# A four-stage transformer stack on one core: stages without barriers, ordered by one list scheduler, with query and key stacks made by products

## The chip, the cores and the metric

The kernel runs on one core of one Trainium2 chip. The metric is the device time of one execution in microseconds (us). A core has a matrix engine (TensorE; PE in the profile, PEld for its weight loads), VectorE (DVE), ScalarE (ACT), GpSimd (POOL) and SyncE (SP, which here only issues DMAs). Each engine works through its own instructions in the order in which the build put them, and waits where one of them waits.

## The reference

Input x is (4, 512, 128) in fp32. Four residual layers follow each other; each batch of 512 tokens (a "block") is independent of the others but for the experts' capacity, which counts tokens over all blocks.

```
x = x + attention(layernorm(x)) @ WO        # 16 heads of 8, causal softmax
x = x + moe(layernorm(x))                   # 8 experts, 2 of them per token, 128 -> 512 -> 128, gelu, capacity
y = layernorm(x) with gain and shift        # recurrence, of layernorm(x) again
state = sigmoid(decay) * state + k * v      #   1024 channels, along the 512 tokens
x2 = xn + (sigmoid(g) * q * state / 8) @ Wo + bo
x = x + x2 + gelu(layernorm(x2) @ W1 + b1) @ W2 + b2
out = x + ternary(layernorm(x))             # silu(w1 y) * (w2 y), two gelu layers of 512x512, w3
```

(xn is layernorm(x); the last layer's weights are −1, 0 or 1 and have a scale for each output.)

## The kernel before, in words

The work of a block is cut into stages, each a Python generator that issues a piece of work at every step and yields an estimate of its cost in us. They are, for a block b:

- `project(b)`: layernorm, four transposes, then the query and key products (`pqk`, one of [128 x 512] each). For the scores the values are wanted as a high and a low part (`hl`, L197 and L198), and stacked by groups of four heads at 32 rows each. The stacking is done by DMA: four DMAs write the parts to DRAM (`rows_q`, `rows_k`, L201) and eight read them back as `qs` and `ks` (L207, L208).
- `maxima(g)`, for each of four head groups: scores on TensorE, the causal mask added by a product with an identity, maxima on VectorE (`mx`, L244), split into two parts (`mh`, L251 and L252) and transposed (`pm`, `mT`).
- `Weights.group(g)`: the scores again with the maxima subtracted by a product with `spread`, exp on ScalarE (`ex`, L283), the diagonal tiles masked on GpSimd (L288), and the products with the values (`po`). `finish` copies `po` (`oT`, L306), transposes it and divides.
- `output(b)`: the product with WO, added to `xs`. `route(b)`: layernorm, router product, the two best experts, each token's row in a buffer of 8 x 192 seats (`rt_at`, L430), and eight indirect DMAs on GpSimd that scatter the tokens to `xgd` in DRAM (L434).
- `experts(b)`: loads `xgd` (`xg`, L472), 12 transposes, then 8 experts of two layers (`ph`, `hT`, `py`, `xoT`), weights loaded through three buffers (`ew`); the results go to DRAM (`ygd`, L500); after a yield of 4.0 eight indirect gathers fetch them (`got`, L536), and after a yield of 6.0 eight VectorE instructions add them to `xs` (L544).
- `recurrence(b)`: two layernorms, then eight channel chunks of four products (`pp`), a scan along the tokens (L605) and an output product (`por`). Its five matrices stay in SBUF (`lk`, `lv`, `lg`, `lq`, `lo`, 512 KB each).
- `feed(b)` and `ternary(b)`: the two feed-forward layers. `ternary` splits its inputs into a high and a low part (`hh`, `hl`, L683 and L684). `round_weights` converts the ternary weights once and looks for values that are not exact (L752 to L760).

The order of instructions comes from `weave`, which takes the next step of whichever of two or three generators has the least estimated time behind it. Stages are woven within two kinds of phase. The experts phase of block b holds experts(b), feed and ternary of block b−1 (for b = 0 `round_weights`) and the maxima of block b+1. The weights phase holds recurrence(b) beside weights, output and route of block b+1 and project(b+2). Each phase opens a tile pool of its own (`phase()`), whose buffers reuse the space of the phase before: a first user of such a buffer waits for the last user of that space. DMAs are issued on SP in program order; scatters and gathers on GpSimd.

TensorE's products and transposes are issued by two helpers, so their lines in the profile are L64 and L67 throughout. The word "(3 forms)" in a group's row means that the shapes differ within it.

Of the kernel before, what the change touches and what calls it, by code (L numbers as in the profile page):

```python
# [20 lines left out]
P = 128  # L21
# [22 lines left out]
def block_kernel(ctx: ExitStack, tc: tile.TileContext, i: dict, out: bass.AP):  # L44
    nc = tc.nc

    const = ctx.enter_context(tc.tile_pool(name="const", bufs=1))
    state = ctx.enter_context(tc.tile_pool(name="state", bufs=1))
    wpool = ctx.enter_context(tc.tile_pool(name="wpool", bufs=1))
    small = ctx.enter_context(tc.tile_pool(name="small", bufs=4))  # L50
    work = ctx.enter_context(ExitStack())
    ypool = work.enter_context(tc.tile_pool(name="ypool", bufs=2))
    att = work.enter_context(tc.tile_pool(name="att", bufs=2))
    stk = work.enter_context(tc.tile_pool(name="stk", bufs=1))
    ew = work.enter_context(tc.tile_pool(name="ew", bufs=3))
    rt = work.enter_context(tc.tile_pool(name="rt", bufs=1))
    scr = work.enter_context(tc.tile_pool(name="scr", bufs=NB, space=DRAM))
    ps_s = work.enter_context(tc.tile_pool(name="ps_s", bufs=2, space=PSUM))
    ps_o = work.enter_context(tc.tile_pool(name="ps_o", bufs=1, space=PSUM))
    ps_d = work.enter_context(tc.tile_pool(name="ps_d", bufs=2, space=PSUM))  # L60
# [8 lines left out]
    class At:  # L69
        pass  # L70

    At.ypool, At.ps_d, At.ew, At.scr = ypool, ps_d, ew, scr

    def bank(name, tag="pt", shape=(P, S)):

        return At.ps_d.tile(list(shape), F32, tag=tag, name=name, bufs=2 if tag == "pt" else 1)
# [18 lines left out]
    mhalf = const.tile([P, TB], F32, name="mhalf")  # L95
# [4 lines left out]
    make_identity(nc, identb)  # L100

# [8 lines left out]
    def layernorm(src, dst):  # L110

        st = small.tile([P, TB, 6], F32, tag="ln_st", name="ln_st")
        mv = small.tile([P, TB, 2], F32, tag="ln_mv", name="ln_mv")
        ve = small.tile([P, TB], F32, tag="ln_ve", name="ln_ve")
        rs = small.tile([P, TB], F32, tag="ln_rs", name="ln_rs")
        for t in range(TB):
            nc.vector.bn_stats(st[:, t, :], src[:, t, :])
        for t in range(TB):
            nc.vector.bn_aggr(mv[:, t, :], st[:, t, :])
        nc.vector.tensor_scalar(ve, mv[:, :, 1], EPS, None, ALU.add)  # L120
        nc.gpsimd.tensor_tensor(rs, ve, mhalf, ALU.pow)  # L121
        for t in range(TB):
            nc.vector.tensor_scalar(
                dst[:, t, :], src[:, t, :], mv[:, t, 0:1], rs[:, t : t + 1],
                ALU.subtract, ALU.mult,
            )

# [10 lines left out]
    def normed(src):  # L138
        y = At.ypool.tile([P, TB, D], F32, tag="y", name="y")
        layernorm(src, y)  # L140
        return y

    def turned(y, gain=None, shift=None):

        yT = At.ypool.tile([P, S], F32, tag="yT", name="yT", bufs=3)
# [6 lines left out]

    def run(stage):
        for _ in stage:
            pass

    def weave(*streams):

        live = [[0.0, n, stage, stretch] for n, (stage, stretch) in enumerate(streams)]
        while live:  # L160
            first = min(live, key=lambda x: x[:2])
            took = next(first[2], None)
            if took is None:
                live.remove(first)
            else:
                first[0] += took * first[3]
# [8 lines left out]
    qs = [stk.tile([P, S], F32R, name=f"qs{g}") for g in range(NG)]  # L175
    ks = [stk.tile([P, S], F32R, name=f"ks{g}") for g in range(NG)]

    mhs = [stk.tile([P, TB, NG, HP], F32R, name=f"mh{x}") for x in range(2)]

    spread = stk.tile([P, P], F32R, name="spread")  # L180

    vs = stk.tile([P, TB, H0, HP], F32, name="vs")

    def project(b, big):

        y = normed(blk(xs, b))
        yield 5.0
        yT = turned(y)
        yield 1.5
        pqk = ps_s.tile([P, 2, S], F32, tag="s", name="pqk")  # L190
        mm(pqk[:, 0, :], lhsT=wq, rhs=yT, start=True, stop=True)
        yield 0.9
        mm(pqk[:, 1, :], lhsT=wk, rhs=yT, start=True, stop=True)
        hl = big.tile([P, 2, 2, S], F32R, tag="hl", name="hl", bufs=1)
        rows = []
        for x, n in enumerate("qk"):
            nc.scalar.copy(hl[:, x, 0, :], pqk[:, x, :])  # L197
            nc.vector.tensor_tensor(hl[:, x, 1, :], pqk[:, x, :], hl[:, x, 0, :], ALU.subtract)  # L198
            d = scr.tile([P, 2, 2, S], F32, tag=f"rows_{n}", name=f"rows_{n}")
            for half in range(2):  # L200
                nc.sync.dma_start(  # L201
                    d[:, half] if n == "q" else d[:, :, half],
                    hl[:, x, half].bitcast(F32).unsqueeze(1).to_broadcast([P, 2, S]),
                )
            rows.append(d.rearrange("(g h) a b s -> g (h a b) s", g=NG))
        for g in range(NG):
            nc.sync.dma_start(qs[g].bitcast(F32), rows[0][g])  # L207
            nc.sync.dma_start(ks[g].bitcast(F32), rows[1][g])  # L208
        yield 0.9
# [4 lines left out]
        yield 1.0  # L214
# [11 lines left out]
    def maxima(g):  # L226

        mx = att.tile([P, TB, NG], F32, tag="mx", name="mx")
        for part in ((3,), (2,), (1, 0)):
            pq = quad()  # L230
            at = 0
            for t in part:
                product(pq, qs[g][:, ts(t, P)], ks[g], 0, (t + 1) * P, at, start=(at == 0))
                at += (t + 1) * P
            at = 0
            for t in part:
                for h in range(NG):
                    mm(pq[h // 2][:, h % 2, at + t * P : at + (t + 1) * P], lhsT=identb, rhs=mask_q,
                       start=False, stop=True, skip_group_check=True)
                at += (t + 1) * P  # L240
            at = 0
            for t in part:
                for pr in range(2):
                    nc.vector.tensor_reduce(  # L244
                        mx[:, t, ts(pr, 2)], pq[pr][:, :, at : at + (t + 1) * P], AX.X, ALU.max,
                        negate=True,
                    )
                at += (t + 1) * P
            yield 1.6
        mh = mhs[g % 2]  # L250
        nc.vector.tensor_copy(mh[..., 0], mx)  # L251
        nc.vector.tensor_tensor(mh[..., 1], mx, mh[..., 0], ALU.subtract)  # L252
        yield 1.0
        pm = bank("pm", shape=(P, TB, P))
        for t in range(TB):
            transpose(pm[:, t, :], mh[:, t].rearrange("p h r -> p (h r)").bitcast(F32))
        mT = mTs[g] = att.tile([P, S], F32R, tag="mT", name="mT", bufs=NG)
        nc.scalar.copy(mT, flat(pm))
        yield 0.5

    mTs = {}

    class Weights:


        def __init__(self, big):
            self.big, self.late = big, None
            self.o = att.tile([P, TB, D], F32, tag="o", name="o", bufs=1)

        def group(self, g):  # L270
            po = ps_o.tile([P, S], F32, tag="po", name="po")
            exs = {}

            def unit(part):
                pq = quad()
                at = 0
                for t in part:
                    product(pq, ks[g][:, ts(t, P)], qs[g], t * P, S, at, start=(at == 0))
                    product(pq, spread, mTs[g], t * P, S, at)
                    at += S - t * P  # L280
                for pr in range(2):
                    ex = self.big.tile([P, 2, S], F32, tag="ex", name="ex", bufs=4)
                    nc.scalar.activation(ex[:, :, :at], pq[pr][:, :, :at], AF.Exp, scale=scale0)  # L283

                    step = S - part[0] * P
                    e = ex.rearrange("p j (i n) -> p j i n", n=step if len(part) > 1 else S)
                    e = e[:, :, : len(part), 0:P]
                    nc.gpsimd.affine_select(  # L288
                        out=e, in_=e, compare_op=ALU.is_ge, fill=0.0, base=0,
                        pattern=[[0, 2], [0, len(part)], [1, P]], channel_multiplier=-1,  # L290
                    )
                    at = 0
                    for t in part:
                        exs[t, pr] = ex[:, :, at : at + S - t * P]
                        at += S - t * P

            def values(t):
                for h in range(NG):
                    mm(po[ts(h, HP), t * P :], lhsT=vs[:, t, NG * g + h, :],
                       rhs=exs[t, h // 2][:, h % 2, :], start=(t == 0), stop=(t == TB - 1))  # L300

            def finish():
                values(2)
                values(3)
                oT = att.tile([P, S], F32, tag="oT", name="oT", bufs=1)
                nc.scalar.copy(oT, po)  # L306
                yield 2.0
                pt = flip(tiles(oT)).rearrange("p t (h r) -> p t h r", r=HP)
# [664 lines left out]
```

## Time and profile before

| | |
|---|---|
| time, median of 4 runs | 899.92 us (895.85 to 900.70) |
| the profiled execution: its own time | 907.21 us |
| its span, from the first to the last instruction | 905.1 us |
| mean granted TensorE clock | 0.824 |
| TensorE busy | 645.9 us (71%) |
| TensorE weight loads | 367.2 us (41%) |
| VectorE busy | 424.7 us (47%) |
| ScalarE busy | 276.7 us (31%) |
| GpSimd busy | 170.0 us (19%) |
| moved by DMA | 56.85 MB, 63 GB/s over the span |

The busy time of an engine counts its arithmetic only. The chain is the sequence of work that ended last, followed back from the last instruction; its shares add up to the span. A line such as "L244 DVE ... mx<-s" names the kernel's line, the engine, and which buffer was made from which. A wait is written as who waited, for whom, the total in us, how often, and the longest.

### The profile page before, as it was taken

Reading aid. Unit: us, or ns where it says so; the run is one execution under the profiler, and the core shown is the slowest. Engines: PE = TensorE matmul, PEld = TensorE weight load, DVE = VectorE, ACT = ScalarE, POOL = GpSimd, SP = SyncE. Lnnn points to the kernel's source line nnn. Section 1 sums busy time; section 2 is a strip of 40 time slices with the busy share of each in tenths; the row PEclk is TensorE's granted clock in tenths of the full one; section 3 lists DMA queues with packets and bytes.
Section 4 is the critical chain, followed back from the end, with each engine's and each line's share of the span. In section 5 each row is a group of like instructions: output and inputs, shape, how many; then the busy total and the mean of one; then the engine's idle time right before and its main releaser. Section 6 shows DMA issues by size and latency. Waiting matters only on the chain.

```text
span 905.1 us, 9226 instructions
## 1 busy us (share of the span) xinstructions
PE 645.9 (71%) x3290; PEld 367.2 (41%) x3290; DVE 424.7 (47%) x1050; ACT 276.7 (31%) x461; POOL 170.0 (19%) x233
## 2 busy tenths in 40 slices
PE   2247852864699619977899439885898397899676
PEld 1123431752234306754334226653334166543244
DVE  3233234536246631587147522595248305657264
ACT  1012430420563104422552114322652054123212
POOL 5001214333221210030221400031220400400100
PEclk8555695876799958999699859998899699799769
DMA  9710025542000162420000162410000122000000
GB/s 258 266 48 0 1 96 183 171 123 56 1 1 13 38 206 59 131 56 1 13 1 12 47 197 79 135 33 12 1 1 12 58 79 73 23 12 0 0 0 16
DMA packets 60102, 56.85 MB, mean 63 GB/s; under 512 B 8336, under 2 KB 43664, under 8 KB 60048
## 3 DMA queue, kind: packets, MB, share of 16 engines
q1 hardware_dynamic: 56720, 49.09, 17.8%
q0 software_dynamic: 2752, 6.82, 2.6%
q8 instruction: 28, 0.46, 0.2%
q10 hardware_dynamic: 576, 0.26, 0.1%
q14 instruction: 26, 0.21, 0.1%
HBM read 37.81 MB, written 18.35 MB: 62 GB/s over the span
## 4 chain that ended last, share of the span: by engine, by line
PE 40%; DVE 19%; issue 15%; POOL 9%; DMA 8%; ACT 7%; SPq 1%; ACTq 0%; POOLq 0%; DVEq 0%
PE pp L64 10%; PE ph L64 6%; PE s L64 6%; DVE mx L244 5%; PE po L64 4%; POOL xgd L434 3%; PE py L64 3%; PE pt L67 3%; ACT ex L283 3%; POOL ln_rs L121 2%; PE por L64 2%; DMA rows_k<-hl 2%; PE pf L64 2%; POOL got L536 1%; POOL stage L755 1%
## 5 line engine op out<-in xcount | busy, mean ns | idle before, releaser
L244 DVE TENSOR_REDUCE mx<-s 128x2 f32<-128x1024 f32 (+3 forms) x128 | 98.3, 818 | 100.3 <-PE s L64 97.9
L283 ACT ACTIVATE ex<-s 128x768 f32<-128x768 f32 (+1 forms) x96 | 79.4, 879 | 73.9 <-PE s L64 73.7
L64 PE MATMUL s<-ks,qs 32*128 32x512 f32 (+3 forms) x256 | 40.2, 500 | 79.9 <-DMA ks<-rows_k 56.6
L288 POOL TENSOR_SCALAR_AFFINE_SELECT ex<-ex 128x256 f32<-128x256 f32 (+1 forms) x96 | 49.5, 516 | 207.3 <-ACT ex L283 206.5
L121 POOL TENSOR_TENSOR ln_rs<-ln_ve,mhalf 128x4 f32<-128x4 f32 x24 | 24.7, 1031 | 254.2 <-DVE ln_ve L120 254.2
L64 PEld LDWEIGHTS s<-ks,qs 32*128 32x128 f32 x256 | 19.2, 242 | 102.0 <-DMA ks<-rows_k 37.6
L64 PE MATMUL ph<-xT,ew 128*128 128x192 f32 x256 | 57.8, 362 | 3.4 <-ACT xT L481 1.3
L64 PE MATMUL ph<-hh,r_h_w 128*128 128x512 f32 x128 | 55.7, 436 | 5.8 <-DVE hh L683 4.6
L64 PE MATMUL ph<-hl,r_h_w 128*128 128x512 f32 x128 | 54.4, 425 | 4.5 <-DVE hl L684 3.3
L64 PE MATMUL py<-hT,ew 128*128 128x192 f32 x256 | 49.1, 336 | 11.6 <-DVE xoT L491 11.6
L521 ACT ACTIVATE hT<-ph,w_mb 128x192 f32<-128x192 f32 x128 | 45.9, 418 | 35.0 <-PE ph L64 33.7
L64 PE MATMUL po<-ex,vs 128*32 128x128 f32 (+3 forms) x512 | 54.3, 517 | 0.9 <-POOL ex L288 0.8
L64 PEld LDWEIGHTS ph<-xT,ew 128*128 128x128 f32 x256 | 46.3, 209 | 11.5 <-ACT hT L521 4.8
L64 PEld LDWEIGHTS py<-hT,ew 128*128 128x128 f32 x256 | 43.1, 194 | 15.2 <-DVE xoT L491 13.6
L603 DVE SCALAR_TENSOR_TENSOR kv<-pp,w_bv,k 128x512 f32<-128x512 f32 x32 | 23.9, 747 | 53.1 <-PE pp L64 53.1
L536 POOL DMA_INDIRECT got<-ygd,rt_at x32 | 31.5, 986 | 86.5 <-DMA ygd<-og 77.9
L64 PE MATMUL s<-qs,ks 32*128 32x512 f32 (+3 forms) x256 | 34.8, 450 | 14.2 <-ACT ex L283 9.4
L724 ACT ACTIVATE h<-ph,w_h_s 128x512 f32<-128x512 f32 x32 | 22.0, 689 | 72.6 <-PE ph L64 69.0
L434 POOL DMA_INDIRECT xgd<-y,rt_at x32 | 31.4, 980 | 65.8 <-DVE wall L454 27.4
L491 DVE TENSOR_SCALAR xoT<-py,w_mb 128x192 f32<-128x192 f32 x32 | 13.3, 415 | 57.7 <-PE py L64 57.7
L605 DVE TENSOR_TENSOR_SCAN st<-dec,kv 128x512 f32<-128x512 f32 x32 | 39.4, 1232 | 0.7
L64 PE MATMUL pp<-yT,w_lq 128*128 128x512 f32 x64 | 36.8, 658 | 1.8 <-DVE kv L603 1.7
(189 smaller groups left out, 1106.5 us busy)
## 6 DMA issues: line engine op xcount, KB each, us to landing
ew<-in_E_dram SPq DMA_DIRECT2D x64, 256.0 KB, 2.9
rows_q<-hl SPq DMA_DIRECT2D x8, 512.0 KB, 2.8
rows_k<-hl SPq DMA_DIRECT2D x8, 512.0 KB, 4.7
qs<-rows_q SPq DMA_DIRECT2D x16, 256.0 KB, 4.0
ks<-rows_k SPq DMA_DIRECT2D x16, 256.0 KB, 3.7
xg<-xgd SPq DMA_DIRECT2D x4, 768.0 KB, 6.3
ygd<-og SPq DMA_DIRECT2D x16, 192.0 KB, 2.1
stage<-in_h_w_dram SPq DMA_DIRECT2D x2, 1024.0 KB, 5.4
```

The lines of the kernel that those rows point to most:

```text
L64: return tc.keep_in_program_order(nc.tensor.matmul(*args, **kwargs))
L67: tc.keep_in_program_order(nc.tensor.transpose(dst, src, ident))
L121: nc.gpsimd.tensor_tensor(rs, ve, mhalf, ALU.pow)
L244: nc.vector.tensor_reduce(mx[:, t, ts(pr, 2)], pq[pr][:, :, at : at + (t + 1) * P], AX.X, ALU.max, negate=True,)
L283: nc.scalar.activation(ex[:, :, :at], pq[pr][:, :, :at], AF.Exp, scale=scale0)
L288: nc.gpsimd.affine_select(out=e, in_=e, compare_op=ALU.is_ge, fill=0.0, base=0, pattern=[[0, 2], [0, len(part)], [1, P]], channel_multipli ...
L434: put = nc.gpsimd.indirect_dma_start(xgd[b % 2], bass.IndirectOffsetOnAxis(at[:, t, k : k + 1], 0), y[:, t, :], None,)
L521: nc.scalar.activation(h[:, j, :], ph[:, j, :], AF.Gelu, bias=mb1[:, c : c + 1])
L536: nc.gpsimd.indirect_dma_start(got[:, t, k, :], None, ygd[b % 2], bass.IndirectOffsetOnAxis(ats[b][:, t, k : k + 1], 0),)
L603: nc.vector.scalar_tensor_tensor(kv, pv, col(bv), k, ALU.add, ALU.mult)
L605: nc.vector.tensor_tensor_scan(st, col(dec).to_broadcast([P, S]), kv, 0.0, ALU.mult, ALU.add)
L724: nc.scalar.activation(h, ph, AF.Gelu, scale=s[:, o : o + 1])
```

## The change

- There are no phases. All buffers come from pools that live through the whole kernel, by tag; tiles that lived in one phase share a tag with others of the same stage (`xg`, `og` and `got` one buffer; `qst` is computed in `oc`, `kv` in `k`, `xoT` in `xT`).
- `play` replaces `weave`: all stages of all blocks are given to one list scheduler at build time. Each stage has a start on a common time line, which acts as its priority, and a stretch. A generator yields a pair (TensorE cost, latency until its next step may come), or the name of a stage or mark that it waits for, or a mark that it has reached.
- `project` makes the stacks by products: `wide` holds each column of WQ and WK four times, eight products of [128 x 512] give queries and keys at four copies per value, ScalarE rounds to the high part, and VectorE leaves in each row the high or the low part by a mask (`lower`). The row DMAs are gone.
- `maxima` transposes `mh` once per block for b > 0 instead of once per group. `po` is one tile for the whole kernel, and its copy `oT` is made on VectorE. In experts, `py` uses one of the two banks that rotate (tag `pt`).
- The recurrence's matrices are not resident: each chunk of channels loads five pieces of 64 KB (`fetch_rec`) into one of three buffers (`rw`), 160 loads in all. Its two layernorms share their statistics.
- `round_weights` goes in 14 pieces of at most 128 x 512. The small parameters are loaded before the stages. The yields around the gathers are gone. The copy of `xs` to `xad` is issued in `route`.

The core of the diff:

```diff
     def project(b, big):
-        hl = big.tile([P, 2, 2, S], F32R, tag="hl", name="hl", bufs=1)
-        for x, n in enumerate("qk"):
-            nc.scalar.copy(hl[:, x, 0, :], pqk[:, x, :])
-            nc.vector.tensor_tensor(hl[:, x, 1, :], pqk[:, x, :], hl[:, x, 0, :], ALU.subtract)
...
-        for g in range(NG):
-            nc.sync.dma_start(qs[g].bitcast(F32), rows[0][g])
-            nc.sync.dma_start(ks[g].bitcast(F32), rows[1][g])
+        wide = two("wide")
+        for x, w in enumerate((wq, wk)):
+            nc.vector.tensor_copy(
+                wide[:, x, :].rearrange("p (n r) -> p n r", r=4), w.unsqueeze(2).to_broadcast([P, D, 4])
+            )
+        for g in range(NG):
+            for x, dst in enumerate((qs[g], ks[g])):
+                pqk = bank("pqk")
+                mm(pqk, lhsT=wide[:, x, ts(g, P)], rhs=yT, start=True, stop=True)
+                hi = At.ff.tile([P, S], F32R, tag="hh", name="hi")
+                nc.scalar.copy(hi, pqk)
+                nc.vector.scalar_tensor_tensor(dst, hi, lower[:, x : x + 1], pqk, ALU.mult, ALU.add)
+                yield 0.86, 0.0
+            yield [f"project{b}.{g}"]
...
+    def play(stages):
+        now, through = 0.0, {}
+        live = {n: [0.0, start, stretch, stage, None] for n, (start, stretch, stage) in stages.items()}
+        while live:
+            for x in live.values():
+                if x[4] in through:
+                    x[0], x[4] = max(x[0], through[x[4]]), None
+            free = [n for n in live if live[n][4] is None]
+            soon = min((live[n][0] for n in free if live[n][1] < 0), default=1e9)
+            if now < soon < now + 0.6:
+                now = soon
+            begin = max(now, min(live[n][0] for n in free))
+            n = min((n for n in free if live[n][0] <= begin), key=lambda n: live[n][1])
+            now, x = begin, live[n]
+            piece = next(x[3], None)
+            if piece is None:
+                through[n] = x[0]
+                del live[n]
+            elif isinstance(piece, str):
+                x[4] = piece
+            elif isinstance(piece, list):
+                through[piece[0]] = now
             else:
-                first[0] += took * first[3]
+                now += piece[0]
+                x[0] = now + piece[1]
+                x[1] += piece[0] * x[2]
...
     experts:
-        yield 4.0
-        got = moe.tile([P, TB, 2, D], F32, tag="got", name="got", bufs=1)
+        got = At.moe.tile([P, TB, 2, D], F32, tag="xg", name="got")
         for t in range(TB):
             for k in range(2):
                 nc.gpsimd.indirect_dma_start(...)
-        yield 6.0
...
+    def fetch_rec(n):
+        if n < NB * NCC and n not in rws:
+            c = n % NCC
+            w = rws[n] = At.rw.tile([P, 5, P], F32, tag="rw", name="rw")
+            for x, src in enumerate("kvgq"):
+                nc.sync.dma_start(w[:, x, :], i["W" + src][:, ts(c, P)])
+            nc.sync.dma_start(w[:, 4, :], i["Wo"][ts(c, P), :])
...
-    for b in range(NB + 1):
-        with phase() as big:
-            streams = []
...
-            weave(*streams)
+    stages = {"round": (0.0, 1.0, round_weights())}
+    for b in range(NB):
+        at = 140.0 * b
+        stages[f"project{b}"] = (-4e3, 1.0, project(b))
+        stages[f"maxima{b}"] = (max(at - 145.0, 0.0), 3.5, maxima(b))
+        stages[f"weights{b}"] = (-5e3 if b else 1.0, 1.0, weights(b))
+        stages[f"output{b}"] = (-5e3, 1.0, output(b))
+        stages[f"experts{b}"] = (at, 1.3, experts(b))
+        stages[f"recurrence{b}"] = (at + 60.0, 1.0, recurrence(b))
+        stages[f"feed{b}"] = (at + 158.0, 1.4, chain(feed(b), ternary(b)))
+    play(stages)
```

The waits by name are: project(b) after weights(b−1); weights(b) after its maxima, experts(b−1) and feed(b−2); output(b) after weights(b); experts(b) after output(b) and experts(b−1); recurrence(b) after experts(b) and recurrence(b−1); feed(b), with ternary(b) behind it, after recurrence(b), output(b+1) and feed(b−1). They order the build; on the chip an instruction waits for its data and its buffers.

## The prediction

> **What bounds the kernel now.** I read the busy shares first, then the long waits, then the windows with the granted clock, and last the chain through one hand-over between stages.
>
> ```profile
> PE 645.9 (71%) x3290; PEld 367.2 (41%) x3290; DVE 424.7 (47%) x1050; ACT 276.7 (31%) x461; POOL 170.0 (19%) x233
> PE 40%; DVE 19%; issue 15%; POOL 9%; DMA 8%; ACT 7%; SPq 1%; ACTq 0%; POOLq 0%; DVEq 0%
> ```
>
> No engine is full. TensorE leads with 646 of 905 us, so 259 us of it are idle, and on the chain of work it carries only 40%. The time is lost where stages meet.
>
> ```profile
> PE s L64 <- DMA ks<-rows_k: 56.6, 4, 19.5
> POOL got L536 <- DMA ygd<-og: 77.9, 4, 22.4
> 300.00:320.00 20.00, 10.66 (x35) 5.09 (x34) 9.13 (x46) 2.55 (x4) 8.85 (x9) 0.85 0.15 52
> 320.00:340.00 20.00, 4.35 (x21) 2.68 (x22) 8.13 (x11) 0.59 (x1) 1.30 (x2) 0.50 0.69 223
> ```
>
> In the windows the first count after the length is TensorE's busy time and the last three are granted clock, DMA share and GB/s. Between 300 and 340 us TensorE works 15 of 40 us; 500–540 is the same (8.35 and 5.83 busy). The chain there says why:
>
> ```profile
> 318.02 0.97 POOL xgd L434
> 319.02 1.06 POOL ln_rs L121
> 321.31 0.85 DVE y L123 x3
> ...
> 324.13 4.87 DMA rows_k<-hl
> ...
> 331.37 7.48 DMA xg<-xgd
> 338.90 2.92 PE pt L67 x12
> ```
>
> The next block's projection has its layernorm queued on GpSimd behind eight scatters (309–319), then goes through DRAM, and the experts' load xg is issued on SP behind those row DMAs. Block 2's hand-over has no projection and is shorter: 14.7 us from the last product of its attention to its experts' input, against 33 and 35 us for blocks 0 and 1's successors.
>
> The span splits as follows (us, from the starts of first scores, last po, xg landing and first ex): head 34; maxima and weights of block 0 87; output and route to xg 37; experts phase E0 75, weights phase W0 73 and hand-over 33; E1 91, W1 75, hand-over 35; E2 92, W2 74, hand-over 15; E3 80; last recurrence 41; tail 62. Sum 904.
>
> **Part by part.**
>
> *Stacks from products.* Gone: four round trips (56.6 us of TensorE waiting: 19.5 in the head, 17.7 and 17.7 in the hand-overs, the rest short), 12 row DMAs per block (48) and their SP issues (0.42 each). Added: 32 products of 128x512 for 8. Row: pqk took (5.4 + 5.0)/8 = 1.30 us per product in mixed clock; the recurrence's pp about 0.9 in dense stretches. So 24 x 0.9 to 1.3 = 22 to 31 us of TensorE. ScalarE: 24 more hi copies x 0.586 = 14. VectorE: 32 combined operations at the kv row's 0.747 against 8 x 0.687, +18; eight wide copies, nearest row vs 0.677, +5. In the head (b = 0) the first scores must now wait for two products, two copies and two combinations instead of 16 us of DMA, but on ScalarE and VectorE the small loads' consumers (dec, s1h) stand between the first groups, and dec's loads took 12 us to land in the head; so I give the head no gain: 34 to 40, taken 39. For blocks 1 to 3 the products stand behind attention of the block before, beside route's VectorE chain.
>
> *No barriers.* In the new order project's layernorm stands before the previous block's attention on GpSimd, so the 10 us of scatter no longer delay it, and xg has no row DMAs before it on SP. The recurrence, which ran beside weights, is now mainly behind them: it fills scatter and xg landing. Weights alone ran at 9.1 us per group (102.4 to 111.1 to 120.6, block 0's last two), woven with recurrence at 13.2. So W costs 4 x 9.1 = 37 us, and then output, route and recurrence. VectorE there: eight channels of kv 0.747 + scan 1.232 + qst 0.750 + oc 0.685 = 27 us, eight stack operations 6, route and its layernorm about 19, together 52; TensorE: 8 x 4.61 (a channel at full clock) + 8 products + 3 = 49. I take 49 for the rest, so 86 per W and hand-over, where before has 106, 110 and 89. For block 0 the SP order puts two channels' weights behind the wait for xg: +8, so 94. The last has no projection: 84. Gain 12 + 24 + 5 = 41.
>
> *Block 0.* Weights may follow each group's maxima. The reduces that look for odd weights (6.6 us as five instructions, now fourteen) stand among the first maxima on VectorE, and the rounding itself on GpSimd before the first select. I take last po at 117 (121.5 before): phase 78. Hand-over 37 as before. E0 loses the rounding, and the next maxima start beside route. First ex comes after hand-over and experts, 37 + 49 = 86 us after last po, or with a gather (below) in front of the last maxima 86 + 21 = 107, against 111 before; taken 98, so E0 is 61.
>
> *Experts phases 1 and 2.* Here the change gives something back. Before, the yield of 6.0 between issuing the eight gathers and the eight applies kept other streams' work between them in all engines' order; it is gone, and in VectorE's order all eight applies (got, L544 before) stand ahead of ternary's first a. VectorE waits in order, so ternary stalls for ygd's landing 2.1, eight gathers of 0.986 with 0.30 between them (10.2) and a last landing of about 2.5: 15 us, plus 6 to refill. Experts alone take 49 us (158 to 207, block 0); ternary's a chain 12 and its hidden layers 20 are read in the tail (865 to 877 to 897). That is 49 + 15 + 6 + 12 + 20 = 102 us if nothing overlaps, and 83 with the gather covered and 2 of slack (before 91 and 92). I take 92, since in before's E2 the same applies cost little and in E0 (got 210.7 to 222) they left TensorE idle for most of 17 us. E3 has ternary's first product pairs ahead of the applies: 80 less a barrier's 4 (the idle gap at 627.8 was 4.85), 76.
>
> *160 small loads instead of five resident matrices.* Each channel now loads five pieces of 64 KB in 512-byte rows through three buffers. A set can be issued only when the output product of channel c−1 is done, which is at the end of channel c, and is needed one channel (4.61 us) later. Nearest rows: 64-KB loads under the head's traffic 3.0 to 4.8 us, 256-KB ew loads in the same phases 2.9. With 2.9 + 0.43 for the issue it is just covered; at 4.8 it costs 0.6 x 32 = 20 us. I take nothing, and keep 20 for the range. The Trainium skill ("DMA: Bandwidth & Descriptors", Rules for kernel authors) speaks against this edit: many small transfers should be coalesced, and under 64 KB one pays mostly overhead; its table gives 0.95 us for 64 KB, so five in a row would be 4.75 us by an estimate from that page, about one channel.
>
> *Small.* 36 transposes fewer for mT (0.11 each, 4 us of TensorE); oT goes from ScalarE to VectorE, 16 x about 0.68 = 11 us, after each group's last po; the recurrence's two layernorms are folded into one (eight statistics, 0.28 and 0.154 each, and one GpSimd hop of 1.03 per block). All beside other work. With its cover gone, oT costs (0.68 − 0.59) x 16 = 1.4 us. VectorE ends near 425 + 35 = 460, still far from the bound.
>
> *Sum.* 39 + 78 + 37 + 61 + 94 + 92 + 86 + 92 + 84 + 76 + 41 + 62 = 842, and 2 outside the span: 844 against the profiled execution's 907.2. That one was 0.8% above the median of the runs (899.9), so 837 on their scale.
>
> **Rivals.**
>
> (A) *The gather is no longer hidden.* Phases E1 and E2 at the full 102: 842 + 20 = 862; with the small loads' 20 too, 882, on the runs' scale 857 to 877. For: 77.9 us of GpSimd waiting for ygd, and VectorE's new order. Against: E2 before.
>
> (B) *The small loads throttle the recurrence: slower.* If they land as the small loads in the head did (8.5 to 12 us), each channel lacks 4.3 to 7.8 us, 32 times: 138 to 250, giving 982 to 1094 for a profiled execution. It eats the whole gain from 63/32 = 2 us per channel on, which is a landing of 6.2 us, as xg has (6.3, but for 768 KB). Against: ew lands 256 KB in 2.9 in these phases, with DMA at 0 to 2 tenths in most slices; only beside xg and ew is it full.
>
> (C) *TensorE-bound.* If the list order fills everything, E1 and E2 are 83, each W 37 + 37 (eight channels) + 6 = 80 with no SP stall, and E0 86 − 37 = 49: 842 − 18 − 24 − 12 = 788, or 784 on the runs' scale.
>
> (D) *The clock.* Weights alone stay at half clock. From 62.3 to 100 us TensorE had no gap over 1.6 us, and the granted clock was 0.50 throughout; two groups and two maxima took 102.4 − 63.7 = 38.7, and with 6.5 per maxima (mx and mh rows) taken off a group took 12.9. (12.9 − 9.1) x 12 = 46, so 888, on the runs' scale 883. The Trainium skill ("TensorE: Matmul & The Clock Gate", HAM oscillation) lays the half clock to idle gaps over about 3.4 us and lets some 3.4 us of sustained work lift it; by that rule weights alone run at full clock and the sum stands. The row of 62 to 100 us contradicts it, so (D) stays open.
>
> (E) *It does nothing*: shared tags and one bank for two tenants order the stages as the barriers did, and products cost what the round trip did: 900.
>
> **How the numbers follow.** The sum has 0.43 (810 to 857), (A) 0.20, (C) 0.18 (770 to 810), (D) 0.06, (B) 0.10, (E) 0.03. The range from 775 to 900 leaves out (B) and the low edge of (C). Half a per cent, about what a measurement of this kernel can tell from no change, is 4.5 us. The sum, (A), (C) and (D) are faster, 0.87; (E) is 0.03 the same; (B) is 0.10 slower.
>
> **What would show it.** Right: no wait of TensorE on row DMAs, the xg load issued within a microsecond of the last scatter, weights groups 9 to 10 us apart, W with hand-over 84 to 94. (A): VectorE waiting for got over 10 us per block with TensorE idle. (B): pp waiting for rw. (D): clock 0.50 in weights. I am wrong if TensorE's idle time stays near 259 us, or if the experts phases last over 102.

## The result, and the profile after

The changed kernel takes 899.52 us (median, 895.18 to 902.83) against 901.58 us for the kernel before: ratio 0.9973, 95% interval 0.9963 to 0.9983. It is faster by 0.3%, not by 7%. The profiled executions (896.0 and 907.2 us) differ by more than the medians, so stages are compared within profiles, and whole kernels by timed ratios.

Engines and chain of the changed kernel, from its page:

```profile
PE 667.9 (75%) x3302; PEld 368.2 (41%) x3302; DVE 455.3 (51%) x1090; ACT 279.7 (31%) x460; POOL 175.3 (20%) x241
...
PE 38%; issue 18%; DVE 16%; POOL 10%; ACT 9%; DMA 7%; SPq 1%; POOLq 0%; ACTq 0%; DVEq 0%
```

TensorE has 22 us more to do and 226 us of idle time instead of 259. Its longest waits, in the same order of columns as before (who, for whom, total, times, longest):

```profile
PE s L71 <- DVE mx L292: 43.2, 33, 7.7
PE pa L71 <- DVE a L803: 28.0, 12, 7.8
...
PE pt L74 <- DMA xg<-xgd: 12.9, 2, 7.3
...
PE pp L71 <- DMA rw<-in_Wk_dram: 8.6, 1, 8.6
```

The wait for row DMAs, 56.6 us, is gone, as forecast. In its place stand waits for VectorE: the maxima, and ternary's first elementwise work `a`. Stage by stage (us; a stage goes from one landmark to the next, as in the prediction; here xg is the start of its first transpose):

| | before | forecast | after | products alone | order alone | best |
|---|---|---|---|---|---|---|
| head, to first scores | 34.0 | 39 | 39.4 | 30.1 | 45.8 | 23.9 |
| block 0, to last po | 87.5 | 78 | 89.8 | 84.0 | 93.6 | 74.5 |
| hand-over 0, to xg | 36.7 | 37 | 45.4 | 49.8 | 36.9 | 42.3 |
| E0, to first ex | 74.6 | 61 | 65.5 | 73.0 | 66.4 | 62.4 |
| W0 and hand-over | 106.1 | 94 | 100.5 | 102.7 | 93.5 | 83.4 |
| E1 | 91.1 | 92 | 102.4 | 89.5 | 101.7 | 93.2 |
| W1 and hand-over | 107.4 | 86 | 81.5 | 103.2 | 82.8 | 85.4 |
| E2 | 94.2 | 92 | 100.5 | 92.2 | 101.7 | 92.5 |
| W2 and hand-over | 90.1 | 84 | 79.5 | 90.1 | 78.2 | 81.2 |
| E3, to recurrence 3 | 80.1 | 76 | 84.1 | 79.9 | 84.0 | 80.3 |
| recurrence 3 and tail | 103.3 | 103 | 105.7 | 102.5 | 105.3 | 103.0 |
| span | 905.1 | 842 | 894.3 | 897.0 | 889.9 | 822.1 |

W1 and W2 brought what was forecast and more. The experts phases, W0, the first hand-over and block 0 took it back.

### The profile page after: what moved, and what is told of

Same layout as the page of the kernel before. It is cut to its first block, busy times and chain, and to the rows that moved or that the text cites. A ratio compares the mean times of both kernels' runs of the same rounds, so it can differ in the third digit from the quotient of the medians.

```text
span 894.3 us, 9476 instructions
## 1 busy us (share of the span) xinstructions
PE 667.9 (75%) x3302; PEld 368.2 (41%) x3302; DVE 455.3 (51%) x1090; ACT 279.7 (31%) x460; POOL 175.3 (20%) x241
## 4 chain that ended last, share of the span: by engine, by line
PE 38%; issue 18%; DVE 16%; POOL 10%; ACT 9%; DMA 7%; SPq 1%; POOLq 0%; ACTq 0%; DVEq 0%
PE ph L71 8%; PE pp L71 7%; PE s L71 7%; DVE mx L292 5%; PE py L71 4%; ACT ex L336 3%; POOL got L599 3%; POOL xgd L497 3%; PE po L71 3%; PE pt L74 3%; PE por L71 2%; PE pf L71 2%; DMA dec<-in_decay_logit_dram 1%; PE pa L71 1%; POOL ln_rs L149 1%
## 5 line engine op out<-in xcount | busy, mean ns | idle before, releaser
L71 PE MATMUL pp<-yT,rw 128*128 128x512 f32 x256 | 132.2, 630 | 14.7 <-DMA rw<-in_Wk_dram 8.6
L71 PEld LDWEIGHTS pp<-yT,rw 128*128 128x128 f32 x256 | 42.9, 192 | 80.2 <-issue 29.6
L149 POOL TENSOR_TENSOR ln_rs<-ln_rs,mhalf 128x4 f32<-128x4 f32 x16 | 18.6, 1162 | 200.1 <-DVE ln_rs L148 121.1
L555 DVE TENSOR_SCALAR xT<-py,w_mb 128x192 f32<-128x192 f32 x32 | 13.3, 416 | 83.0 <-PE py L71 82.9
L71 PE MATMUL po<-ex,vs 128*9 128x256 f32 (+3 forms) x512 | 54.2, 501 | 1.7 <-POOL ex L341 1.6
L497 POOL DMA_INDIRECT xgd<-y,rt_at x32 | 36.6, 1143 | 94.5 <-DVE rt_at L493 63.4
L71 PE MATMUL s<-qs,ks 32*128 32x512 f32 (+3 forms) x256 | 41.4, 437 | 18.3 <-ACT ex L336 9.5
L71 PE MATMUL pqk<-yT,wide 128*128 128x512 f32 x64 | 37.4, 712 | 18.2 <-DVE ks L253 9.4
L71 PEld LDWEIGHTS ph<-xT,ew 128*128 128x128 f32 x256 | 41.0, 190 | 14.3 <-ACT hT L585 4.6
L359 DVE COPY oT<-po 128x512 f32<-128x512 f32 x16 | 11.0, 690 | 66.7 <-PE po L71 66.7
```

The lines of the kernel that those rows point to most:

```text
L71: return tc.keep_in_program_order(nc.tensor.matmul(*args, **kwargs))
L149: nc.gpsimd.tensor_tensor(rs[:, 0, :], rs[:, 0, :], mhalf[:, 0, :], ALU.pow)
L359: nc.vector.tensor_copy(oT, po)
L497: put = nc.gpsimd.indirect_dma_start(xgd[b % 2], bass.IndirectOffsetOnAxis(at[:, t, k : k + 1], 0), y[:, t, :], None,)
L555: nc.vector.tensor_scalar(xT[:, ts(e, SEATS)], py, mb2[:, e : e + 1], None, ALU.add)
```

## The experiments

**The two parts, each alone.** Products in the kernel before, phases and `weave` untouched:

```diff
     def project(b, big):          # kernel before
-        # two products, hl, twelve row DMAs
+        # wide, eight products, hi, scalar_tensor_tensor as in the change
```

> The kernel before with one part of the change alone: the stacks of queries and keys come from eight products per block instead of the way through DRAM; phases and order as before. Theory S (the round trip was worth 17 to 19 us at two hand-overs and 16 in the head, and the products take 10 to 15 us in its place, in route's way): 15 to 35 us faster, ratio 0.96 to 0.985. Rival (in the hand-overs the scatter and the load of the experts' input end last, so the round trip was hidden, and the products come on top): ratio 0.995 to 1.01.

Ratio 0.9957 (0.9932 to 0.9982): 0.4%, within the rival's range. W0 and W1 fell by only 3.4 and 4.2 us though a wait of 17.7 us in each was gone, and hand-over 0 grew by 13.1. The rival's reason is not what the trace shows, though. In W0 the experts' input landed at 329.9 us, 9 us earlier than before, and its first transpose came only at 339.6: the stack products, their VectorE operations and the first scores stood ahead of it from 326.9 us on. W1 is alike (521.8 and 532.3). So the products took up the time that the row DMAs had left.

The order alone, with the stacks through DRAM as before:

```diff
     def project(b):               # changed kernel
-        # wide, eight products, hi, scalar_tensor_tensor
+        # two products, hl, twelve row DMAs
```

> The changed kernel without its other part: the stacks go through DRAM again as in the kernel before, in the new order without phases. Theory S2 (the round trip through DRAM lay mostly beside the scatter and the way of the experts' input, 56.6 us of waiting notwithstanding: with products alone in the old order the hand-overs fell only by 3 to 5 us): 0 to 10 us slower than the changed kernel, nearly all of it in the head, ratio 0.997 to 1.008. Rival T (the round trip's 17 us per block are TensorE's wait and come back in full): 35 us slower or more, ratio over 1.03. Third (the products cost more than the DMAs in route's way): ratio below 0.99.

Ratio 0.9903 (0.9874 to 0.9932): faster than the changed kernel, next to the third expectation; theory S2 missed. So the order is worth 1.0% by itself, the products 0.4%, and both together 0.3%. In the new order the hand-overs have no row wait over a microsecond:

```profile
PE s L71 <- DMA ks<-rows_k: 29.8, 1, 29.8
```

One wait is left, the head's, where nothing else can run; the other three are filled by the recurrence.

**Products out of route's way.** First the whole of project, then its products alone, behind route of the block before:

```diff
-            yield f"weights{b - 1}"
+            yield f"output{b - 1}"        # first
...
+        if b > 0:
+            yield f"routed{b - 1}"        # second: before the products;
+                                          # route yields this mark after its scatters
```

> The changed kernel, but project of a block is ordered behind output and route of the block before it, not beside them. Theory P (the eight stack products on TensorE and their eight copies and eight VectorE operations stand in between route's short steps and lengthen the way from the last attention product to the scatter: 28.4 us for block 0 and 34, 33, 29 for the others against 20.1 for block 0 before): block 0's way falls to 20 to 22 us and the others by about 6; the hand-over of block 0 by 8. As the maxima move behind, E0 gets up to 5 longer; in all 8 to 20 us faster than the changed kernel, ratio 0.975 to 0.99. Rival (those steps only fill time in which the chain waits anyway): scatter no earlier than 27 us after the last product, ratio 0.995 to 1.005.

> The changed kernel, but the eight stack products of a block wait in the order until route of the block before has issued its last product; the layernorm and the transposes stay where they are, so that the products fill the scatter and the load of the experts' input. With the whole of project behind route the scatter of block 0 came 20.5 us after the last attention product instead of 28.4, but project's layernorm then stood on GpSimd behind the eight scatters and TensorE idled 19 us. Theory P: scatter of block 0 at 20 to 21 us and the others 1 to 3 us earlier than in the changed kernel, no idle gap over 8 us after it, 6 to 14 us faster, ratio 0.982 to 0.991. Rival (the maxima behind the products then come later by as much, and they end the experts phase of block 0): ratio 0.995 to 1.000.

The first: 1.013 (1.0096 to 1.0164), slower. The scatter of block 0 came 20.5 us after the last po instead of 28.4, as theory P says, the others 2.3 us earlier at most; but project's layernorm stood on GpSimd behind the scatters and TensorE was idle 19.2 us in that hand-over; E0 and E2 came out 15 us longer each. The second kept the layernorm in front: 0.9823 (0.9787 to 0.9859), 1.5% better than the changed kernel, scatter of block 0 after 21.7 us, hand-over 0 down to 39.0 and W0 to 91.5. Theory P holds once nothing else of the stage is moved with it.

**The gather's cover.** A yield between gathers and applies, and the applies pinned in VectorE's order where the build has them:

```diff
                     bass.IndirectOffsetOnAxis(ats[b][:, t, k : k + 1], 0),
                 )
+        yield 0.0, 22.0
...
-                nc.vector.scalar_tensor_tensor(x, got[...], wks[b][...], x, ...)
+                tc.keep_in_program_order(nc.vector.scalar_tensor_tensor(...))
```

What it undoes, in the chain of the changed kernel's E1 and in VectorE's timeline (start, length, instruction, and in brackets idle time before it and its releaser):

```profile
396.28 0.94 POOL got L599
...
397.53 2.63 DMA got<-ygd,rt_at
...
400.25 0.35 DVE xs L606
...
402.69 1.68 POOL ln_rs L670
...
404.40 1.11 DVE y L139 x4
405.52 0.59 DVE a L803
...
409.30 0.80 PE pa L71
```
```profile
400.25 0.35 DVE L606 SCALAR_TENSOR_TENSOR xs<-got,rt_wk,xs 128x128 f32<-128x128 f32 x1 [0.86 <-DMA got<-ygd,rt_at]
...
404.40 1.11 DVE L139 TENSOR_SCALAR y<-xs,ln_mv,ln_rs 128x128 f32<-128x128 f32 x4 [1.47 <-POOL ln_rs L670]
405.43 0.68 DVE L803 SCALAR_TENSOR_TENSOR a<-a,pa 128x512 f32<-128x512 f32 x1
```

The first `a` (405.43) has had its product since 399.5. It stands behind the applies, which wait for the gathers, and behind the recurrence's layernorm, which needs the last apply and then a power on GpSimd. TensorE was idle 4.24 and 5.85 us and worked at half clock for 34 us:

```profile
380.00:400.00 20.00, 11.06 (x73) 7.38 (x70) 13.62 (x39) 1.50 (x3) 8.68 (x9) 0.67 0.27 76
400.00:420.00 20.00, 11.57 (x25) 6.39 (x25) 16.04 (x48) 2.90 (x5) 2.68 (x2) 0.50 0.00 0
```

> The changed kernel with one thing undone: between the eight gathers of an experts phase and their eight applies other stages get 22 us of the order again, and the applies are pinned in VectorE's order where the build put them, behind the ternary stage's first products and first hidden layer. Theory G (the applies standing ahead of ternary's first elementwise work on VectorE leave TensorE idle for 10 us and at half clock afterwards in each of the experts phases 1 to 3): those phases go from 102.4, 100.5 and 84.1 us to about 90, 88 and 80, no wait of TensorE over 4 us stands before pa, and the ratio to the kernel before is 0.965 to 0.975. Rival R (the phases are bounded by TensorE's and VectorE's work whatever the order, and what is gained here is given back because the recurrence starts later): phases shorter but the weights phases longer by as much, ratio 0.99 to 1.00.

Ratio 0.9867 (0.9828 to 0.9907), between the two expectations. E1, E2 and E3 fell to 94.0, 93.2 and 81.4: theory G's direction, less than its size. E0, which theory G leaves out, fell most, from 65.5 to 53.2: in the changed kernel the applies stand there ahead of the next block's maxima, and the wait of 7.7 us for `mx`, the longest of its row in the list above, is gone. But W1 grew from 81.5 to 101.8. Part of it is what rival R says: 12 of the recurrence's 64 products, which in the changed kernel stand at the end of E1 (from 434.7 us to the first ex at 443.0), now come behind it. Another part is a wait for the recurrence's loads. Of the two waits in this line, 8.5 us are in W1 and 5.2 in W0:

```profile
PE pp L71 <- DMA rw<-in_Wk_dram: 13.7, 2, 8.5
```

**One more buffer for the small loads,** alone and with the cover:

```diff
-    pools(work, "", y=1, moe=1, ew=3, rec=2, rw=3, ff=8, p_d=1)
+    pools(work, "", y=1, moe=1, ew=3, rec=2, rw=4, ff=8, p_d=1)   # and sets fetched three ahead
```

> The changed kernel with four buffers for the recurrence's small loads instead of three, each set fetched one channel earlier. Theory L (of the 160 loads only the two sets of block 0 that stand on SP behind the wait for the experts' input cost time: one wait of 8.65 us on TensorE in the profile): that wait falls below 3 us, 3 to 8 us faster than the changed kernel, ratio 0.988 to 0.996. Rival (landing throttles every channel): 1 us or more in each of 32 channels, ratio below 0.97. If neither, 0.997.

> The gather covered again as in the first experiment, and four buffers for the recurrence's loads. With the cover alone the experts phases fell by 8.4, 7.3 and 2.7 us, but the second hand-over grew by 20 (81.5 to 101.8 from first ex to the experts' input), with TensorE 8.55 us idle before pp for the loads that stand on SP behind the wait for the experts' input. Theory H (that wait is what gave the gain back): with the loads one set earlier no wait of TensorE on rw is over 3 us, the second hand-over falls to 85 to 93, and the whole is 10 to 18 us faster than with the cover alone, ratio 0.967 to 0.976. Rival R (the recurrence only starts later, because its input comes later, and its work has to go somewhere): second hand-over stays at 97 or more, ratio 0.983 to 0.988.

Alone 0.9921 (0.9887 to 0.9955), half a per cent; with the cover 0.9729 (0.9679 to 0.9779). Both ratios lie in the ranges of theories L and H. Of their signs less holds: a wait of 4 us on rw is left in each, and W1 fell only to 96.0, between H's 85 to 93 and rival R's 97. So the wait on SP explains 6 of the 20 us by which the cover had lengthened W1; W0 gained as much, 101.4 to 94.7. What SP does without the buffer stands in the changed kernel's chain: the last scatter lands, SP issues xg, and the recurrence's loads only behind it.

```profile
317.11 2.72 DMA xgd<-y,rt_at
...
320.03 0.38 SPq L539
...
320.50 4.83 DMA rw<-in_Wk_dram
...
325.47 3.58 PE pp L71 x4
```

**All three, then the head.** The three together, and with them the decay and four other small operations moved from the head to behind experts 0; the third kernel has the DMAs in place of the products:

> Gather covered, four buffers for the small loads, and the stack products behind route's last product, all three together. Theory (three separate waits, one in the experts phases, one at SP, one in the hand-over: their gains add): 0.9729 for the first two, and the third alone took 1.5% off the changed kernel, so 0.955 to 0.962, 861 to 867 us. Rival (they share a bound, since a stage that ends sooner meets the next wait): 0.965 to 0.973.

> The same, and five small operations on parameters (the decay's tanh on ScalarE and four on VectorE) are put behind the first experts phase, where in the changed kernel they stand among the stack products of block 0. Theory W (they wait for the last small loads of the head, and the products behind them with them: two idle gaps of TensorE of 5.1 and 8.3 us): both gaps fall below 2 us, first scores at 28 to 31 us instead of 39, 8 to 11 us faster than without. Rival (the first maxima then wait for something else that comes late, the odd-weight reduces on VectorE behind GpSimd's rounding): first scores earlier, but first exp still at 55 or later, less than 4 us faster.

> Gather covered, four buffers, small operations late, but the stacks through DRAM as in the kernel before. Theory S2 (in the hand-overs the round trip lies beside scatter and experts' input; the products are worth their price only in the head, where nothing covers the round trip): the hand-overs as with the products behind route, the head 12 to 16 us longer, 0.958 to 0.967, which is 8 to 16 us slower than its counterpart with products. Rival (products cost more than they save everywhere): faster than its counterpart.

Together 0.9559 (0.9522 to 0.9596): the gains add. The small operations: 0.9555 (0.9519 to 0.9590), nothing. Theory W fell and its rival held: the first scores came at 24.2 instead of 38.5, and then TensorE waited 18.1 us, because on VectorE the odd-weight reduces stood ahead of the first maxima and waited for GpSimd's rounding:

```profile
PE s L71 <- DVE mx L294: 20.0, 4, 18.1
DVE odd L858 <- POOL stage L857: 18.8, 9, 11.9
```

The kernel with DMAs: 0.9434 (0.9400 to 0.9469), 1.2% better than its counterpart with products although its last po of block 0 comes 11.6 us later. My theory S2 fell. The W stages with their hand-overs, products (first) and DMAs (second); first count TensorE busy:

```profile
218.90:312.70 93.80, 81.41 (x427) 34.13 (x427) 54.69 (x136) 38.97 (x55) 24.04 (x35) 0.95 0.15 43
404.80:495.90 91.10, 79.50 (x426) 33.26 (x427) 50.24 (x114) 38.87 (x54) 21.95 (x33) 0.96 0.16 44
```
```profile
230.30:315.30 85.00, 75.10 (x414) 32.06 (x415) 48.95 (x128) 35.47 (x49) 24.94 (x35) 0.94 0.30 94
404.00:489.40 85.40, 75.28 (x414) 32.00 (x415) 44.57 (x107) 35.36 (x48) 23.60 (x33) 0.93 0.28 90
```

TensorE is 87 to 88% busy there, and the products' 6.3 and 4.2 us of it are most of the 8.8 and 5.7 us by which these stages are longer. Here, where the recurrence fills the hand-over, added work was paid for, and taking the row DMAs' wait away brought nothing. E1 and E2 were also 3.4 and 4.2 us shorter with the DMAs; the reason for that is open.

**Products in block 0 only; rounding behind the first route.**

```diff
-        wide = two("wide")
+        if b == 0:
+            # wide, eight products ...
+        else:
+            # two products, hl, twelve row DMAs ...
...
     def round_weights():
+        yield "output0"
...
-                nc.gpsimd.tensor_copy(rw[key][:, c, :], w)
+                tc.keep_in_program_order(nc.gpsimd.tensor_copy(rw[key][:, c, :], w))
```

> Gather covered, four buffers, small operations late, and the stacks by products in block 0 only, through DRAM for blocks 1 to 3. Theory Q (a product costs its 0.87 us of TensorE wherever TensorE or VectorE has work to do, which in the new order is also so in the hand-overs; only the head has nothing else to do during the round trip): the head and block 0 as with products (last po at 127 to 130), the weights phases with hand-over as with the DMAs (85 to 86 us), and 8 to 13 us faster than with DMAs in all four blocks, ratio 0.928 to 0.935. Rival (what the DMAs gained came from elsewhere, such as the order that the scheduler happened on): within 4 us of the DMAs, 0.938 to 0.947.

> The same, and the rounding of the ternary weights is ordered behind the first route, its casts pinned behind the first scatters on GpSimd. Theory O (with the small operations out of the way the first maxima still stood on VectorE behind the odd-weight reduces, the first of which came at 35.9 us and waited for GpSimd's rounding of weights that land late in the head): TensorE's 18.1 us gap after the first scores goes, first exp at 38 to 44 us instead of 57, and 12 to 18 us faster, ratio 0.910 to 0.920. Rival (the first gather of block 0 then stands behind the casts on GpSimd, 14 times 1.9 us, and the experts phase of block 0 gives it back): less than 5 us faster.

Mixed: 0.9372 (0.9328 to 0.9417), against 0.9434 with DMAs throughout. By stages it is as theory Q says (last po at 128.2, the W stages 83.4 and 85.4); the ratio is short of its range, between it and the rival's, and the two intervals overlap a little. With the rounding later 0.9192 (0.9154 to 0.9230): theory O; first ex at 37.1 instead of 56.4, the 18 us gap gone. Of the 19 us won at last po, block 0's hand-over and E0 gave back 12 (GpSimd now rounds there), and E1 came out 4 longer, so that the two profiled executions are only 2.4 us apart where the medians are 14; the ratio above goes by the medians.

**The clock in block 0.** 48 products per group that nobody reads, in block 0's maxima:

```diff
+                if b == 0:
+                    fill = bank("fill", "sum")
+                    for j in range(16):
+                        mm(fill[:, 0:P], lhsT=identb, rhs=mask_q, start=True, stop=True)
```

> The changed kernel with work added and none taken out: in block 0's maxima each of the three parts of a group is followed by 16 small products that nobody reads (128x128, 48 per group, about 0.06 us each at full clock and 0.12 at half). Theory D (from 42 to 120 us the granted clock is at half nearly throughout because no stretch of 3.4 us is fully busy, and TensorE at half clock sets the group's period of 20.6 us): the clock rises to 1.0 within that stretch, the period falls to 14 to 17 us, and the phase from first scores to last po from 89.8 to 70 to 80; ratio 0.978 to 0.99. Rival (the period is set by the chain from scores through VectorE and ScalarE, or the clock does not follow such products): period 22 to 27, phase 95 to 110, ratio 1.003 to 1.02.

> The same with the 192 useless products in block 0's maxima. Alone they took 5 us off the phase from first scores to last po and let the clock rise for stretches of 10 us. Theory D: 3 to 7 us faster than without them; rival (the phase is now bounded by VectorE's odd-weight reduces in the first group and the chain in the others): within 2 us.

> The same with the 192 useless products in block 0's maxima. Theory D (half the clock, not the chain, sets block 0's period of 20 us per group): the clock rises in stretches, last po 4 to 8 us earlier, ratio 0.004 to 0.009 lower than without. Rival (with the first maxima freed the groups follow each other so closely that the clock is up without them): no gain, or up to 4 us lost.

Ratios 0.9913 (0.9884 to 0.9942), 0.9495 (0.9453 to 0.9537) and 0.9137 (0.9084 to 0.9191), each 0.6% better than its counterpart (0.9973, 0.9555, 0.9192); in the last two pairs the intervals overlap, but the three agree. In the changed kernel theory D's direction came, short of its ranges: block 0 fell by 5 us, not to 80 or less. Added work makes the kernel faster. In the last pair, without (first) and with it (second), the column after the counts being the granted clock:

```profile
60.00:80.00 20.00, 14.69 (x104) 6.71 (x102) 7.66 (x13) 5.31 (x7) 2.56 (x6) 0.59 0.00 1
80.00:100.00 20.00, 15.74 (x120) 7.06 (x118) 7.65 (x13) 4.85 (x8) 2.54 (x5) 0.59 0.00 1
```
```profile
60.00:80.00 20.00, 14.83 (x181) 8.98 (x173) 9.06 (x17) 5.44 (x7) 2.97 (x6) 1.00 0.00 1
80.00:100.00 20.00, 15.46 (x179) 7.77 (x176) 6.08 (x13) 8.47 (x11) 5.09 (x10) 1.00 0.01 2
```

Last po came 5 to 11 us earlier. This last kernel, at 823.9 us, is the best of all: 8.6% faster than the kernel before.

## Why the prediction was wrong

The direction was right, and the mechanisms that take time away are there: no row waits, layernorm ahead of the scatters, recurrence in the hand-over. The sum was 842 us of span and 894.3 were measured. On the scale of the medians the miss is 62 us, 837 against 899.5, because the profiled execution was 0.8% above the median for the kernel before and 0.4% below it for the changed one. The 52 us of span by steps:

- **Experts phases, +27 (E1 10.4, E2 8.5, E3 8.1).** The step that failed was "I take 92, since in before's E2 the same applies cost little". Its own upper end was 102: measured 102.4 and 100.5. The reason for 92 was a reading of the old order, in which the applies stood among other work on VectorE; in the new order they stand ahead of it, which the step itself had found. Covered, the phases took 94.0 and 93.2. Rival (A) was right about the place, and its chance of 0.20 too low. That its 102 was hit so closely is partly luck: it has no recurrence in it, and 12 of the recurrence's 64 products for a block stand in E1 and 12 in E2. For E3 the step counted on ternary's first product pairs ahead of the applies and on "a barrier's 4". Two pairs were ahead, and the third waited 7.8 us; the cover took only 2.7 us off, and the rest is open.
- **W1 and W2, −9 against these.** The 12 products each that stand already in the experts phase are missing here, and the weights groups came 7.4 to 8.4 us apart where 9.1 was taken. Their clock was 0.89 to 1.00 (240 to 272, 443 to 473 and 625 to 657 us), so rival (D) did not come there. Taken together, E1 with W1 is 5.9 us over the forecast and E2 with W2 4.0.
- **Block 0, +12.** "I take last po at 117": it came at 129.2. The odd-weight reduces in front of the first maxima were named and not priced: with the rounding moved, in the mixed kernel, the last po came 19 us earlier. The half clock was priced for the weights of the later blocks, but it is block 0 that it rules.
- **First hand-over, +8, and W0, +6.5.** "Hand-over 37 as before" and products "beside route's VectorE chain" at nothing. They were in it: 28.4 us to the scatter instead of 20.1; behind route these two stages took 39.0 and 91.5. W0 also has the SP wait, forecast as +8, measured 8.65.
- **E0, +4.5.** "Taken 98" lay halfway between the gather in front of the last maxima and not; it is in front, and covering it took E0 to 53.2. **The end, +2.7,** is open.
- **The stacks.** "Gone: 56.6 us of TensorE waiting" was a gain only for the head. In the hand-overs of the old order the products took up the time in its place, and the new order fills it with the recurrence; products alone brought 0.4%.
- **The small loads** taken at nothing, 20 kept for the range: one more buffer brought 0.5%, 4 to 5 us. Rival (B) did not come. The Trainium skill warns of many small transfers ("DMA: Bandwidth & Descriptors", Rules for kernel authors). Here the 160 loads of 64 KB cost TensorE one wait of 8.65 us, for their place in the queue behind another load's wait, and no other.
- **The clock rule** of the Trainium skill ("TensorE: Matmul & The Clock Gate", HAM oscillation) was held against the row of 62 to 100 us. Here both parts can be seen. In block 0 of the changed kernel no gap from 60 to 120 us is over 2.3 us, and the clock was at half for all but 7 us of it; it rose when products without purpose filled the short gaps. So short gaps keep the clock down, not those over 3.4 us alone; that sustained work lifts it agrees. Theory D's "no stretch of 3.4 us is fully busy" is not so: stretches of up to 4.6 us had no gap.

## What to carry to other kernels

Taking a wait away gains only the time until the next thing that the stage waits for: ask what ends the stage next, and price added work by the stage in which it will run, not by the one it replaces. When barriers go, the order within each engine's queue becomes the barrier: before dropping a yield or a buffer, list for every engine what stands behind an instruction that waits for a DMA. And two improvements that fill the same gap don't add: the order alone brought 1.0%, the products alone 0.4%, both 0.3%. Run each alone. A stage that gets shorter may only have handed its work to the next; compare the two together.

## What the runs showed of the hardware

TensorE's clock stayed at half for 44 us (28 to 72 us of the kernel with the rounding moved) in which it was busy 70% of the time and had no idle gap over 2.27 us:

```profile
28.00:72.00 44.00, 30.67 (x186) 14.54 (x184) 16.06 (x26) 9.59 (x12) 4.64 (x10) 0.50 0.27 77
```

A stretch of 4.27 us without a gap, from 48.4 us, did not raise it there. In the changed kernel the clock rose at 93.2 us, after 3.4 us without a gap, and was at half again 3.4 us later, though in between TensorE was busy half the time and no gap was over 1.7 us:

```profile
89.79:93.20 3.41, 3.41 (x26) 1.16 (x23) 0.00 (x0) 1.51 (x2) 0.84 (x2) 0.50 0.00 0
93.20:96.60 3.40, 1.71 (x30) 1.15 (x28) 2.33 (x6) 0.27 (x1) 0.00 (x0) 1.00 0.00 0
96.60:113.70 17.10, 13.36 (x82) 5.56 (x75) 5.33 (x7) 5.28 (x7) 2.95 (x6) 0.50 0.00 1
```

And 192 small products that nobody needs paid for themselves three times. The eight scatters took 12.6 us in block 1's hand-over of the changed kernel and 10.0 us in block 0's, with VectorE busy for 9.2 and 6.5 us of it; what slows them wasn't tried.
